# Layer 1 attention masks: from TensorE transposes of loaded tiles to a casting DMA and a transposing DMA

## Chip, cores and metric

The kernel runs on one core of one Trainium2 chip. The metric is the device time of one execution in microseconds (us). Most executions of one kernel agree within 0.3%. The profile is one execution, recorded by the hardware profiler.

Engines are named as in the profile: PE is TensorE (PEld its weight loads), DVE is VectorE, ACT is ScalarE, POOL is GpSimd, SP is SyncE. SP issues most DMAs; POOL issues the indirect ones. Both kinds run on the core's 16 DMA engines.

## The reference, cut to what matters

The model has two layers over `x` (32 batches, 512 nodes, 256 features) and a 0/1 adjacency `adj` (32, 512, 512, int32). Layer 0 is a mean aggregation over `adj` and a feed forward with a max-plus part; layer 1 is a graph attention and a slice mixer. The change is in layer 1's attention:

```
h = einsum("bnd,hde->bhne", nodes, W)                        # 4 heads of 64
e_src, e_dst = (h * a_src), (h * a_dst) summed per type t
weight = sum over t of (node_adj == t + 1) * (e_src[..., :, None] + e_dst[..., None, :])
weight = leaky_relu(weight, 0.01)
weight = where(node_adj == 0, -1e9, weight)
attention = softmax(weight, axis=-1)
dst = einsum("bhij,bhje->bhie", attention, h) + bias
out = layer_norm(relu(dst) + h)
```

With an adjacency of zeros and ones only one type counts, and the softmax is a masked sum: a row i adds over those j where adj[i, j] is 1. The kernel keeps j on the partitions, so it needs the adjacency turned: `mask[j, i] = adj[i, j]`.

## The kernel before, in words

**The fast path and its check.** `tile_kernel` runs `layer0_sorted` and, interleaved with its end, `layer1_plain`. Both assume something of the data and note in the tile `over` where it does not hold. At the end `over` is summed, read into a register as `rows`, and if it is above zero, both layers are computed again by general versions (L2206 to L2208). Layer 1's assumptions on the adjacency are two: it holds zeros and ones only, and no row is empty.

**Order of the work.** The code is written as Python generators that yield between pieces; `woven` and `braid` interleave them. A scheduler then orders the instructions on each engine's queue; each engine takes its queue strictly in order. Layer 0 begins with `features` (a chain of small DVE steps on the feed forward's weights) woven with `convs(0)`, the aggregation of the first 8 batches. Each batch loads four adjacency tiles through SP (L393), POOL turns them into floats (L394), and the layer norm of a batch takes an inverse root on POOL (`deviation`, L30 and L31) before DVE (L46) and ACT (L57) go on. When the features and the first segment are done, the feed forwards begin; layer 1's constants are set up between them (`following`), and from about 2450 us on layer 1 runs alone.

**Layer 1.** `attentions` handles one batch after the other: `attention(b)` is woven with `prepare(b + 1)`, by the counts TURNS - 4 (10) and STEPS (15). These also enter PACE, by which the whole stream is mixed with `mixer`, the second half of the layer, in pairs of batches. `prepare(b)` gathers the batch's nodes by POOL's indirect DMA (L1156), brings in the mask, normalises, turns x (`turned`), computes h and the exponentials (L1182 to L1188), and at its end writes a row per head to DRAM and reads it back broadcast to all partitions (`ownd`, `own`: L1199, L1202, on SP). `weigh` (L1215, DVE) multiplies the larger of `own` and `other` by the mask; `attention` feeds the result to PE (L1248, L1255).

**The mask before.** `masks(b)` loads four tiles of 128 rows (`ai`, int32, two buffers) through SP. For each, ACT makes one pass that casts to bf16 and sums each row (L1095), and a second that squares and sums (L1096). PE turns the four 128x128 blocks of the bf16 tile (`maskp`, L1086), DVE writes them into the mask as uint8 (L1087). The row sums lie in `edges`: the sum of squares equals the sum for zeros and ones, and a sum below 0.5 is an empty row. `masks(0)` runs while layer 0 still works; the others in `prepare(b)`.

Of the kernel before, what the change touches and what calls it, by code (L numbers as in the profile page):

```python
# [10 lines left out]
I32 = mybir.dt.int32  # L11
BF16 = mybir.dt.bfloat16
U32 = mybir.dt.uint32
AF = mybir.ActivationFunctionType
ALU = mybir.AluOpType
# [4 lines left out]
P = 128  # L20
N = 512
D = 256
NT = N // P
# [843 lines left out]
def layer1_plain(tc, ident, eps, x2s, ranks, adj, w, out, over, ps):  # L867
# [3 lines left out]
    nc = tc.nc  # L871
    B = adj.shape[0]
    SEG = B // len(x2s)
    GB = 2
    AH, _, HO = w["W"].shape
# [13 lines left out]
    HE = HO + 1  # L889
    AP = AH // 2  # L890
    TURNS = AP * NT + 6
    STEPS = 15
    WANTED = 68
    AHEAD = 3
    ATT = 2 * (AHEAD + 2) + AP + 1
# [7 lines left out]
    with ExitStack() as ctx:  # L903
        cst = ctx.enter_context(tc.tile_pool(name="c1", bufs=1, side="right", reuse_waits="tile"))
        dr = ctx.enter_context(tc.tile_pool(name="d1", bufs=2, space=DRAM))

        def ctile(name, shape):
            return cst.tile(shape, F32, tag=name, name=name)
# [8 lines left out]

        ones = ctile("ones", [P, P])
        nc.gpsimd.memset(ones, 1.0)
        identb = cst.tile([P, P], BF16, tag="identb", name="identb")  # L920
        nc.vector.tensor_copy(identb, ident)

        wa = ctile("wa", [P, DC, AH * HO + 2 * AH])
        for c in range(DC):
# [17 lines left out]
                                 start=c == 0, stop=c == DC - 1)  # L942
            nc.vector.tensor_scalar(over[:, : 2 * AH], pn[:, : 2 * AH], SMALL, None, ALU.is_gt)
        yield
        edges = ctile("edges", [P, 2, B * NT])
        abias = const("abias", [P, AH * HO], w["gnn_bias"].rearrange("h e -> (h e)").partition_broadcast(P))
        gamma = const("gamma", [P, AH * HO], w["ln_gamma"].rearrange("h e -> (h e)").partition_broadcast(P))
        beta = const("beta", [P, AH * HO], w["ln_beta"].rearrange("h e -> (h e)").partition_broadcast(P))
# [121 lines left out]
            nc.scalar.activation(ebsl, ebsl, AF.Exp)  # L1070

        se = ctx.enter_context(tc.tile_pool(name="e1", bufs=2, side="right", reuse_waits="tile"))
        masked = {}

        def masks(b, bank="any"):

            a, raw = [], []

            def load(t):
                raw.append(se.tile([P, N], I32, tag="ai", name=f"ai{b}_{t}", bufs=2))  # L1080
                nc.sync.dma_start(raw[t], adj[b, t * P : (t + 1) * P, :])

            def turn(t):
                pt = ps.tile([P, NT, P], BF16, tag=bank, name=f"maskp{b}_{t}")
                for j in range(NT):
                    nc.tensor.transpose(pt[:, j, :], a[t][:, j * P : (j + 1) * P], identb)  # L1086
                nc.vector.tensor_copy(mask[:, :, t * P : (t + 1) * P], pt)  # L1087

            load(0)
            load(1)  # L1090
            yield
            for t in range(NT):
                n = b * NT + t
                a.append(se.tile([P, N], BF16, tag="a", name=f"a{b}_{t}", bufs=3))
                nc.scalar.activation(a[t], raw[t], AF.Identity, accum_out=edges[:, 0, n : n + 1])  # L1095
                nc.scalar.activation(raw[t], raw[t], AF.Square, accum_out=edges[:, 1, n : n + 1])  # L1096
                if t + 2 < NT:
                    load(t + 2)
                if t == 1:
                    mask = se.tile([P, NT, N], mybir.dt.uint8, tag="mask", name=f"mask{b}")  # L1100
                    yield
                if t > 1:
                    turn(t - 2)
                    yield
            for t in range(NT - 2, NT):
                turn(t)
                yield
            masked[b] = mask

        yield from masks(0, "mm")  # L1110
        yield True
        ps = ctx.enter_context(tc.tile_pool(name="p1", bufs=4, space=PSUM, reuse_waits="tile"))
        sb = ctx.enter_context(tc.tile_pool(name="s1", bufs=2, reuse_waits="tile"))
# [9 lines left out]
        def normed(xt, xn, name):  # L1123

            mv = sb.tile([P, NT, 2], F32, tag="mv" + name[0], name=f"mv{name}")
            for t in range(NT):
                st = sb.tile([P, 6], F32, tag="st" + name[0], name=f"st{name}_{t}", bufs=4)
                nc.vector.bn_stats(st, xt[:, t, :])
                nc.vector.bn_aggr(mv[:, t, :], st)
            rs = sb.tile([P, NT], F32, tag="rs" + name[0], name=f"rs{name}")  # L1130
            deviation(nc, rs, mv[:, :, 1], eps)
            shift = sb.tile([P, NT], F32, tag="shift" + name[0], name=f"shift{name}")
            nc.vector.scalar_tensor_tensor(shift, mv[:, :, 0], -1.0, rs, ALU.mult, ALU.mult)
            for t in range(NT):
                nc.scalar.activation(xn[:, t, :], xt[:, t, :], AF.Identity, bias=shift[:, t : t + 1],
                                     scale=rs[:, t : t + 1])
# [13 lines left out]
        def prepare(b):  # L1150

            while b >= AHEAD_X and b - AHEAD_X not in stored:
                yield True
            xt = xs[b] = sb.tile([P, NT, D], F32, tag="x", name=f"x{b}", bufs=AHEAD_X)
            for t in range(NT):
                nc.gpsimd.indirect_dma_start(  # L1156
                    out=xt[:, t, :], out_offset=None, in_=x2s[b // SEG],
                    in_offset=bass.IndirectOffsetOnAxis(
                        ap=ranks[:, b * NT + t : b * NT + t + 1].bitcast(U32), axis=0))

            hv = sb.tile([P, NT, AH, HE], F32, tag="hv", name=f"hv{b}")
            xn = hv.rearrange("p t h e -> p (t h e)")[:, : NT * D].rearrange("p (t d) -> p t d", t=NT)
            edged = masks(b) if b not in masked else range(3)
            for i, _ in enumerate(edged):
                if i < 3 or b not in masked:
                    yield
                if i == 2:
                    normed(xt, xn, f"c{b}")
                    nc.gpsimd.tensor_add(xt, xt, beta.unsqueeze(1).to_broadcast([P, NT, D]))
                    yield  # L1170
            mask = masked.pop(b)
            xnT = yield from turned(xn, "x3T", f"x3T{b}")
            yield


            ht = sb.tile([P, NT, AH * HO], F32, tag="ht", name=f"ht{b}")
            other = sb.tile([P, NT, AH], F32, tag="other", name=f"other{b}")
            mine = sb.tile([P, AH, NT], F32, tag="mine", name=f"mine{b}")
            for t in range(NT):
                ph = psum("any", f"hp{b}_{t}")  # L1180
                for c in range(DC):
                    nc.tensor.matmul(ph[:, : AH * (HO + 2)], xnT[:, c, t * P : (t + 1) * P], wa[:, c, :],  # L1182
                                     start=c == 0, stop=c == DC - 1)
                d = ph[:, AH * HO : AH * HO + AH]
                nc.scalar.activation(mine[:, :, t], ph[:, AH * (HO + 1) : AH * (HO + 2)], AF.Exp, scale=1.0 - SLOPE)
                nc.scalar.activation(hv[:, t, :, HO], d, AF.Exp)
                nc.scalar.activation(other[:, t, :], d, AF.Exp, scale=SLOPE - 1.0)
                nc.scalar.copy(ht[:, t, :], ph[:, : AH * HO])  # L1188
                yield

            nc.gpsimd.tensor_add(hv[:, :, :, :HO], ht.rearrange("p t (h e) -> p t h e", h=AH),
                                 abias.rearrange("p (h e) -> p h e", h=AH).unsqueeze(1).to_broadcast([P, NT, AH, HO]))
            yield
            pt = psum("any", f"minep{b}")
            nc.tensor.transpose(pt[: AH * NT, :P], mine.rearrange("p h t -> p (h t)"), ident)
            row = sb.tile([AH * NT, P], F32, tag="turned", name=f"turned{b}", bufs=1)
            nc.scalar.copy(row, pt[: AH * NT, :P])
            own_row = dr.tile([AH, N], F32, tag="own", name=f"ownd{b}")
            nc.sync.dma_start(own_row.rearrange("h (t p) -> (h t) p", p=P), row)  # L1199
            own = [wide("own", f"own{b}_{h}", AH + 1) for h in range(AH)]  # L1200
            for h in range(AH):
                nc.sync.dma_start(own[h], own_row[h].partition_broadcast(P))  # L1202
            for t in range(NT):
                nc.vector.tensor_mul(hv[:, t, :, :HO], hv[:, t, :, :HO], hv[:, t, :, HO:].to_broadcast([P, AH, HO]))
            ready[b] = mask, ht, hv, other, own
            yield
# [11 lines left out]
        def attention(b):  # L1218

            mask, ht, hv, other, own = ready[b]  # L1220
            xt = xs[b]
# [46 lines left out]
            yield  # L1268
            dt = back(dT, "dp")
            rs = sb.tile([P, NT, AH], F32, tag="rs", name=f"rs{b}")  # L1270
            nc.vector.tensor_scalar_max(rs, dt.rearrange("p (t h e) -> p t h e", t=NT, h=AH)[:, :, :, 0], 1e-30)
            nc.vector.reciprocal(rs, rs)
            for q in range(AP):
# [325 lines left out]


        flags = over[:, 2 * AH + 3 :]
        nc.vector.tensor_sub(flags, edges[:, 1, :], edges[:, 0, :])
        nc.vector.tensor_scalar(flags, flags, 0.0, None, ALU.not_equal)
        nc.vector.tensor_scalar(edges[:, 0, :], edges[:, 0, :], 0.5, None, ALU.is_lt)
        nc.vector.tensor_add(flags, flags, edges[:, 0, :])


def layer1(tc, ident, eps, x2, adj, w, out):
# [632 lines left out]
```

## Time and profile before

| | |
|---|---|
| median of 3 runs | 4578.43 us (4575.21 to 4583.15) |
| profiled run | 4587.94 us |
| span of the profile (first to last instruction) | 4586.1 us |
| mean granted TensorE clock | 0.943 |
| layer 1, from 2530 to 4485 us | 1955 us |
| one batch of layer 1, by the distance of the ownd stores | about 63 us |

Lines of the profile that give the kernel's state besides those of the next part:

```profile
PE   5567988889988899878997999999999999999987
...
DVE  6668888887788877777775777777777777777763
ACT  2344565556655555555664444544544444554432
```

Each digit is the busy share of one fortieth of the span, in tenths. Layer 0's opening is the three slices on the left; layer 1 alone starts at about the 22nd. An idle engine costs nothing as such: what counts is which engine or DMA the others wait for in that stage.

### The profile page before, as it was taken

The page shows a single profiled execution, that of the slowest core. Times are in us where ns is not written, and L with a number is a line of the kernel's source. Part 1 is how long each engine was busy: PE and PEld are TensorE (multiplying, and loading weights), DVE is VectorE, ACT ScalarE, POOL GpSimd, SP SyncE. Part 2 cuts the span into 40 slices and gives each one's busy share as a digit, 9 for nine tenths or more (in the row PEclk, how much of TensorE's full clock was granted, in tenths as well). Part 3 has the DMA queues.
Part 4 walks back from the last instruction along what each step waited for, and adds up shares of the span by engine and source line. Part 5 has one row for each costly group of instructions (what it writes and reads, how often), then busy time and mean ns, then how long its engine had stood idle before and what let it go on. Part 6 is the DMA issues. An engine that isn't in the chain of part 4 may idle for free.

```text
span 4586.1 us, 56206 instructions
## 1 busy us (share of the span) xinstructions
PE 4011.0 (87%) x19287; PEld 2462.2 (54%) x19287; DVE 3391.6 (74%) x7008; ACT 2296.8 (50%) x4756; POOL 1743.1 (38%) x2036
## 2 busy tenths in 40 slices
PE   5567988889988899878997999999999999999987
PEld 4444655556556566445554355555555555555555
DVE  6668888887788877777775777777777777777763
ACT  2344565556655555555664444544544444554432
POOL 2356544654535644353423233222232333322210
PEclk8778999999999999989998999999999999999998
DMA  4447533654436543464422111111111111111100
GB/s 135 155 141 224 179 125 118 203 185 141 142 116 197 182 148 119 121 225 158 140 89 69 35 54 47 56 53 41 47 47 51 54 56 54 53 49 56 40 15 15
DMA packets 235100, 474.09 MB, mean 103 GB/s; under 512 B 38299, under 2 KB 114075, under 8 KB 234804
## 3 DMA queue, kind: packets, MB, share of 16 engines
q0 software_dynamic: 80256, 282.38, 19.2%
q1 hardware_dynamic: 154548, 188.02, 13.2%
q8 instruction: 154, 2.52, 0.2%
q14 instruction: 142, 1.16, 0.1%
HBM read 413.16 MB, written 57.16 MB: 103 GB/s over the span
## 4 chain that ended last, share of the span: by engine, by line
PE 28%; DVE 25%; DMA 7%; POOL 7%; issue 7%; ACT 4%; DVEq 0%; POOLq 0%; SPq 0%; ACTq 0%
DVE att L1215 4%; PE avp L1248 3%; PE clsp L625 3%; PE gatep L625 3%; DVE acc L639 2%; DMA rows<-table,xs 2%; DVE sw L1338 2%; PE po L654 2%; PE yTp L1348 2%; DVE sw L1343 2%; PE adp L1255 2%; DVE sst L1341 2%; PE oTp L1536 1%; PE xp L1401 1%; PE zp L1394 1%
## 5 line engine op out<-in xcount | busy, mean ns | idle before, releaser
L625 PE MATMUL clsp<-xnT,wc 128*128 128x512 f32 x1024 | 535.7, 643 | 83.8 <-ACT cls L627 53.2
L625 PE MATMUL gatep<-xnT,wg 128*128 128x512 f32 x1024 | 505.2, 613 | 13.8 <-ACT gate L627 13.5
L654 PE MATMUL po<-wd,acc 128*128 128x256 f32 x2048 | 458.5, 383 | 10.1 <-DVE h L410 7.2
L1215 DVE SCALAR_TENSOR_TENSOR att<-own,other,mask 128x512 f32<-128x512 f32 x512 | 392.3, 791 | 71.9 <-DMA own<-ownd 71.9
L654 PEld LDWEIGHTS po<-wd,acc 128*128 128x128 f32 x2048 | 391.4, 192 | 78.0 <-issue 11.1
L639 DVE SCALAR_TENSOR_TENSOR acc<-past,fld,acc 128x512 f32<-128x512 f32 x448 | 353.8, 794 | 34.0 <-ACT past L638 25.9
L600 DVE SCALAR_TENSOR_TENSOR best<-rows,xs,best 128x1024 f32<-128x1024 f32 x212 | 275.2, 1302 | 127.2 <-ACT best L594 71.5
L625 PEld LDWEIGHTS gatep<-xnT,wg 128*128 128x128 f32 x1024 | 199.5, 199 | 263.2 <-issue 205.7
L638 ACT ACTIVATE past<-tz,fld 128x512 f32<-128x512 f32 x448 | 291.4, 693 | 78.9 <-DVE acc L639 78.0
L597 POOL DMA_INDIRECT rows<-table,xs x212 | 255.3, 1204 | 166.2 <-DVE best L600 117.1
L625 PEld LDWEIGHTS clsp<-xnT,wc 128*128 128x128 f32 x1024 | 187.6, 203 | 241.0 <-issue 125.1
L634 ACT ACTIVATE acc<-tz,fld 128x512 f32<-128x512 f32 x256 | 198.8, 778 | 229.8 <-PE tz L632 229.4
L1348 PE MATMUL yTp<-sw,x 128*128 128x512 f32 x512 | 262.8, 650 | 57.4 <-DVE sw L1343 54.5
L1248 PE MATMUL avp<-att,hv 128*64 128x512 f32 x1024 | 305.0, 618 | 2.3 <-DVE att L1215 2.3
L436 PE MATMUL pm<-h,adj 128*128 128x258 f32 (+1 forms) x1024 | 180.4, 323 | 111.3 <-DVE keep L441 36.1
L1301 POOL TENSOR_TENSOR mu<-mu,eps 128x16 f32<-128x16 f32 x32 | 113.3, 3540 | 389.8 <-DVE mu L1300 389.7
L627 ACT ACTIVATE cls<-clsp,fld 128x512 f32<-128x512 f32 x256 | 175.7, 686 | 160.2 <-DVE acc L643 76.2
L1336 PE MATMUL lgp<-wsl,x4T 128*128 128x512 f32 x512 | 243.9, 610 | 9.3 <-ACT sw L1337 4.3
L1156 POOL DMA_INDIRECT x<-x2s,ranks x128 | 134.0, 1047 | 293.2 <-DVE att L1215 129.5
L627 ACT ACTIVATE gate<-gatep,fld 128x512 f32<-128x512 f32 x256 | 175.6, 686 | 136.5 <-PE gatep L625 102.1
L555 POOL DMA_INDIRECT xs<-rows_of,order x128 | 154.8, 1209 | 231.9 <-DVE acc L639 99.2
L1568 PE MATMUL outp<-v,swT 128*128 128x256 f32 x1024 | 227.6, 381 | 0.0
(599 smaller groups left out, 8943.0 us busy)
## 6 DMA issues: line engine op xcount, KB each, us to landing
adji<-in_adj SPq DMA_DIRECT2D x128, 256.0 KB
ai<-in_adj SPq DMA_DIRECT2D x128, 256.0 KB
own<-ownd SPq DMA_DIRECT2D x128, 256.0 KB
rows_of<-keep SPq DMA_DIRECT2D x32, 550.0 KB
x<-in_x SPq DMA_DIRECT2D x32, 512.0 KB
x2s<-xs SPq DMA_DIRECT2D x32, 512.0 KB
out<-x SPq DMA_DIRECT2D x32, 512.0 KB
rows<-table,xs POOLq DMA_INDIRECT x212
```

What stands on the lines that cost most here:

```text
L597: nc.gpsimd.indirect_dma_start(out=row, out_offset=None, in_=table, in_offset=bass.IndirectOffsetOnAxis(ap=idxs[:, k : k + 1].bitcast(U32) ...
L600: nc.vector.scalar_tensor_tensor(m, row, vals[:, k : k + 1], m, ALU.add, ALU.max)
L625: nc.tensor.matmul(pf, wf[:, c, f * P : (f + 1) * P], xnT[:, c, :], start=c == 0, stop=c == DC - 1)
L627: nc.scalar.activation(o, pf, fn, bias=fld[:, f, bf : bf + 1], scale=1.0 if fn == AF.Gelu else 0.5)
L638: nc.scalar.activation(r, z, AF.Relu, bias=fld[:, f, AT + b : AT + b + 1])
L639: nc.vector.scalar_tensor_tensor(y, r, fld[:, f, CH + b : CH + b + 1], y, ALU.mult, ALU.add)
L654: nc.tensor.matmul(po[:, i, :], acc[f][:, t * P : (t + 1) * P], wd[:, f, :], start=f == 0, stop=f == FC - 1)
L1215: nc.vector.scalar_tensor_tensor(e, own[h], other[:, j, h : h + 1], mask[:, j, :], ALU.max, ALU.mult)
L1248: nc.tensor.matmul(pv[q][k * HO : (k + 1) * HO, :], hv[:, j, h, :HO], weighed[b, h, j], start=j == 0, stop=j == NT - 1)
L1336: nc.tensor.matmul(pf, xnT[:, c, t * P : (t + 1) * P], wsl[:, c, :], start=c == 0, stop=c == DC - 1)
L1348: nc.tensor.matmul(py, xn[:, t, c * P : (c + 1) * P], sw[:, t, :], start=t == 0, stop=t == NT - 1)
L1568: nc.tensor.matmul(po[:, :D], swT[:, k, t * P : (t + 1) * P], v[:, k, :], start=k == 0, stop=k == KC - 1)
```

## The change

The adjacency of a batch is cast to bf16 by a DMA that POOL issues (`shorten`), from DRAM to DRAM, and brought into SBUF turned by a transposing DMA that SP issues (`turn`). The mask is bf16 instead of uint8. In place of ACT's two passes for each tile there is one Square pass for each batch over the whole mask with a bias of -0.5 (its result goes into a buffer that is overwritten later): each zero and each one gives 0.25, so the sum for a partition is 0.25 x 4 x 512. Empty rows are found from the attention's denominators: a denominator that is not above zero. TensorE's transposes, their PSUM tiles, DVE's casts and the bf16 identity are gone. `prepare` has 12 yields instead of 15, and STEPS follows.

```diff
-    STEPS = 15
+    STEPS = 12
...
-        def masks(b, bank="any"):
-            a, raw = [], []
-            def load(t):
-                raw.append(se.tile([P, N], I32, tag="ai", name=f"ai{b}_{t}", bufs=2))
-                nc.sync.dma_start(raw[t], adj[b, t * P : (t + 1) * P, :])
-            def turn(t):
-                pt = ps.tile([P, NT, P], BF16, tag=bank, name=f"maskp{b}_{t}")
-                for j in range(NT):
-                    nc.tensor.transpose(pt[:, j, :], a[t][:, j * P : (j + 1) * P], identb)
-                nc.vector.tensor_copy(mask[:, :, t * P : (t + 1) * P], pt)
...
-                nc.scalar.activation(a[t], raw[t], AF.Identity, accum_out=edges[:, 0, n : n + 1])
-                nc.scalar.activation(raw[t], raw[t], AF.Square, accum_out=edges[:, 1, n : n + 1])
...
-        yield from masks(0, "mm")
+        short, masked = {}, {}
+        def shorten(b):
+            if b < B:
+                short[b] = dr.tile([N, N], BF16, tag="short", name=f"short{b}", bufs=3)
+                nc.gpsimd.dma_start(short[b], adj[b], max_dma_last_dim=8192)
+        def turn(b):
+            if b < B:
+                masked[b] = se.tile([P, NT, N], BF16, tag="mask", name=f"mask{b}")
+                nc.sync.dma_start_transpose(masked[b], short.pop(b))
+        for b in range(2):
+            shorten(b)
+            yield
+        turn(0)
         yield True
...
-            edged = masks(b) if b not in masked else range(3)
-            for i, _ in enumerate(edged):
...
+            if b:
+                turn(b)
+            shorten(b + 2)
+            yield
+            yield
+            yield
+            normed(xt, xn, f"c{b}")
...
             ht = sb.tile([P, NT, AH * HO], F32, tag="ht", name=f"ht{b}")
+            nc.scalar.activation(ht.rearrange("p t e -> p (t e)").bitcast(BF16), mask.rearrange("p t n -> p (t n)"),
+                                 AF.Square, bias=centre, accum_out=edges[:, b : b + 1])
...
             rs = sb.tile([P, NT, AH], F32, tag="rs", name=f"rs{b}")
+            nc.vector.tensor_scalar(edges[:, B + b * NT : B + (b + 1) * NT],
+                                    dt.rearrange("p (t e) -> p t e", t=NT)[:, :, 0], 0.0, None, ALU.is_le)
...
-        nc.vector.tensor_sub(flags, edges[:, 1, :], edges[:, 0, :])
-        nc.vector.tensor_scalar(flags, flags, 0.0, None, ALU.not_equal)
-        nc.vector.tensor_scalar(edges[:, 0, :], edges[:, 0, :], 0.5, None, ALU.is_lt)
-        nc.vector.tensor_add(flags, flags, edges[:, 0, :])
+        nc.vector.tensor_copy(flags, edges[:, B:])
+        nc.vector.scalar_tensor_tensor(flags[:, :B], edges[:, :B], 0.25 * NT * N, flags[:, :B],
+                                       ALU.not_equal, ALU.add)
```

More of the change, by code (lines that the diff above doesn't have):

```diff
@@ L919, in layer1_plain @@
         nc.gpsimd.memset(ones, 1.0)
-        identb = cst.tile([P, P], BF16, tag="identb", name="identb")
-        nc.vector.tensor_copy(identb, ident)
         wa = ctile("wa", [P, DC, AH * HO + 2 * AH])
@@ L944, in layer1_plain @@
         yield
-        edges = ctile("edges", [P, 2, B * NT])
+        edges = ctile("edges", [P, B + B * NT])
+        centre = ctile("centre", [P, 1])
+        nc.gpsimd.memset(centre, -0.5)
         abias = const("abias", [P, AH * HO], w["gnn_bias"].rearrange("h e -> (h e)").partition_broadcast(P))
@@ L1072, in layer1_plain @@
         se = ctx.enter_context(tc.tile_pool(name="e1", bufs=2, side="right", reuse_waits="tile"))
-        masked = {}
-        def masks(b, bank="any"):
-            a, raw = [], []
-            def load(t):
-                raw.append(se.tile([P, N], I32, tag="ai", name=f"ai{b}_{t}", bufs=2))
-                nc.sync.dma_start(raw[t], adj[b, t * P : (t + 1) * P, :])
-            def turn(t):
-                pt = ps.tile([P, NT, P], BF16, tag=bank, name=f"maskp{b}_{t}")
-                for j in range(NT):
[L1086 to L1090, printed above, removed]
-            yield
[L1092 to L1108, printed above, removed]
-        yield from masks(0, "mm")
+        short, masked = {}, {}
[9 more added lines that the diff above has]
+            shorten(b)
+            yield
+        turn(0)
         yield True
@@ L1162, in prepare @@
             xn = hv.rearrange("p t h e -> p (t h e)")[:, : NT * D].rearrange("p (t d) -> p t d", t=NT)
-            edged = masks(b) if b not in masked else range(3)
-            for i, _ in enumerate(edged):
[L1165 to L1170, printed above, removed]
+            if b:
[5 more added lines that the diff above has]
+            normed(xt, xn, f"c{b}")
+            nc.gpsimd.tensor_add(xt, xt, beta.unsqueeze(1).to_broadcast([P, NT, D]))
+            yield
             mask = masked.pop(b)
```

## The prediction

> **What bounds the kernel now.** I read the page first: span, busy shares, DMA queues.
>
> ```profile
> PE 4011.0 (87%) x19287; PEld 2462.2 (54%) x19287; DVE 3391.6 (74%) x7008; ACT 2296.8 (50%) x4756; POOL 1743.1 (38%) x2036
> ```
>
> Then busy time by stage: the first 35 us, the rest of the opening (features and first segment), and layer 1 in its steady part. Columns are length, then busy us of PE, weight loads, DVE, ACT and POOL, then clock, DMA share, GB/s.
>
> ```profile
> 0.00:35.00 35.00, 7.76 (x27) 5.71 (x28) 13.78 (x26) 5.13 (x8) 11.27 (x59) 1.00 0.79 248
> 35.00:345.00 310.00, 194.62 (x903) 154.08 (x902) 219.57 (x801) 123.12 (x254) 120.35 (x290) 0.77 0.44 133
> 2530.00:4485.00 1955.00, 1834.39 (x10615) 1045.38 (x10613) 1426.79 (x3016) 925.47 (x2356) 550.19 (x411) 0.98 0.15 48
> ```
>
> The reader sees two different limits. Layer 1 is PE's (94% busy), DVE second, ACT half idle, DMA almost free. The opening is no engine's: it is short waits in turn, and in its first 35 us the DMA engines are what is full (0.79).
>
> Third, the groups that the change removes (busy us, mean ns):
>
> ```profile
> L1087 DVE CAST mask<-maskp 128x512 uint8<-128x512 bf16 x128 | 85.1, 674 | 2.5 <-PE maskp L1086 2.0
> L1096 ACT ACTIVATE ai<-ai 128x512 int32<-128x512 int32 x128 | 81.6, 639 | 1.3
> L1095 ACT ACTIVATE a<-ai 128x512 bf16<-128x512 int32 x128 | 80.4, 629 | 44.8 <-issue 29.5 <-DMA ai<-in_adj 13.1 <-PE maskp L1086 2.2
> L1086 PE MATMUL maskp<-identb,a 128*128 128x128 bf16 x512 | 46.1, 222 | 6.1 <-ACT sw L1337 3.9 <-DVE mask L1087 1.3 <-ACT a L1095 0.8
> ```
>
> Fourth, the chain of waits in one of layer 1's batches (start, us, what). It alternates: a stretch where DVE decides, then one where PE does.
>
> ```profile
> 3102.45 0.56 DVE mask L1087
> ...
> 3145.62 0.33 PE maskp L1086 x4
> ...
> 3161.19 0.67 PE maskp L1086 x12
> ```
>
> Adding the chain's pieces from 970 us to the end: L1087 30.4 us, L1086 15.5, L1095 with L1096 6.2; together 52.1.
>
> Last, POOL's opening, because the casts go to its queue:
>
> ```profile
> 23.73 0.61 POOL L394 CAST adj<-adji 128x512 fp32r<-128x512 int32 x1 [1.16 <-DMA adji<-in_adj]
> ...
> 27.00 1.27 POOL L394 CAST adj<-adji 128x512 fp32r<-128x512 int32 x2 [1.37 <-DMA adji<-in_adj]
> ...
> 33.93 1.01 POOL L31 TENSOR_TENSOR rsa<-rsa,eps 128x4 f32<-128x4 f32 x1
> ```
>
> POOL makes layer 0's adjacency (L394) and the norm's root (L31) within 35 us; DVE's next layer norm step (L46, 35.02 us) waits for that root, and all that is queued behind it on DVE, the features too, follows.
>
> **What the Trainium skill says.** "DMA: Bandwidth & Descriptors", section "SWDGE vs HWDGE vs iDMA": a cast inside a DMA can only be issued from GpSimd, a transposing DMA only from SP or ACT. The trace has neither. The same page, "Issuing engines are not separate DMA queues": DMAs of all issuers run on the same 16 engines and interleave. The trace agrees: only SP's queue is active in the first 35 us and already fills 0.79. "VectorE: DVE Perf Modes", "The three transpose paths": 1309 ns for a 128x128 bf16 block by DMA; no run shows it yet.
>
> **The change, part by part.**
>
> *Where the casts stand.* I compared the instruction order of the built changed kernel with the old one. The casts depend on nothing but an input, the buffers in DRAM hold none of them back, and the scheduler puts all 32 of them among POOL's first 73 entries, ahead of layer 0's second adjacency. The diff, which writes them into each batch's preparation, does not show this. Eight may be in flight: cast n+8 waits on POOL until cast n has landed. Read off that order: the first rsa (L31) stands behind the landing of cast 8, adj tiles 2 and 3 behind cast 14, the second rsa behind cast 23, the next adj behind cast 24. POOL's issue itself is some 32 x 1.0 us (an indirect DMA takes 1047 ns at L1156), inside those waits.
>
> *Price of a cast (c).* It reads 1.05 MB and writes 0.52 MB. The fullest slices of the opening move 339 to 346 GB/s. Reading alone sets the pace: 1.05/345 = 3.0 us, the lower end. Read and write both count: 1.57/345 = 4.6 us, which I take, as source and target are both in DRAM. The conversion halves the rate: 9.1 us, the upper end; nothing in the trace shows a converting DMA.
>
> *The opening.* The second rsa ends at 34.9 us now. Afterwards: 4 us to the first cast, 0.79 x 35 = 27.7 us of DMA work that the opening needs anyway on the same engines, 23 x 4.6 = 105, and 1 for L31: about 138. That is 103 late. Some waits vanish in it because their loads will have landed (high 4.4 us, sl 1.5): -6. So +97 (62 with c = 3.0; 201 with 9.1). The last 8 casts (36 us of DMA) run beside the feature loads and may add up to 25; I take 0 and keep it for the range. Nothing hides this: PE, DVE and ACT take their queues in order and each has batch 1's layer norm in front of the features; the first feed forward needs both.
>
> *Layer 1, removed.* PE 46.1 us, DVE 85.1, ACT 80.4 + 81.6 plus 25.0 + 25.9 of accumulator reads = 212.9, and 128 loads of 256 KB. Of that 52.1 lay on the chain. What is late next where DVE's cast goes is the next DVE instruction; where PE's turns go, the next matmul. Bounds: 25, if the other engine takes up half; 86, if the freed DVE and ACT also take a third from PE's 120.6 us of idle time (46 + 40).
>
> *Layer 1, added.* 32 ACT squares over 2048 elements: 128x1024 takes 1057 ns at L1297, so about 2.0, with the read 0.2: 70 us in all, 143 less than removed; cover is ACT's 53% idle time; without it up to 2 us each. 32 comparisons on DVE of about 0.15 us: 5, taken as on the chain. The multiplication at L1215 reads bf16 for uint8, with two f32 operands as before (791 ns; L639, all f32, 794): 0. Gain 52 - 5 = 47.
>
> *Transposing DMA.* It stands on SP just ahead of the previous batch's own rows: turn(b+1) before own(b), and waits until DVE's last att of b-1 frees the mask buffer. Queued behind it are ownd and own, and att of b waits for those. The slack is there now:
>
> ```profile
> 3164.88 0.73 DVE L1215 SCALAR_TENSOR_TENSOR att<-own,other,mask 128x512 f32<-128x512 f32 x1
> ```
>
> ```profile
> 3186.80 0.33 SPq L1199 DMA_DIRECT2D ownd<-turned  x1
> ```
>
> 21 us here, 14 to 35 over the batches after the second. Lower end: 0.5 MB at 345 GB/s, 1.5 us; upper: 16 blocks x 1.309 = 21 us (estimate from the page named). Either fits nearly everywhere: 0, at worst 25 in all.
>
> *The rest.* STEPS 15 to 12 keeps the weave, since the preparation now has 12 yields: 0, with 10 either way. The check's sum is exact in f32 (2048 x 0.25 = 512), so the branch that repeats both layers stays untaken.
>
> **Sum.** +97 - 47 = +50. The profiled run took 4587.9 (span 4586.1), giving 4638; the median of the three runs is 4578.4, 9.5 lower, so 4628.
>
> **Rivals.**
> A, faster: the opening has room. If casts go at c = 3.0 and 20 us of the delay are taken up by later DMA waits of the features (wraw 14.3, every 8.0), it costs 42; with a gain of 86 the time is 4534, with 60, 4560. For it: DMA is at 0.44 after 35 us. Against: those waits are for new transfers, not for old ones.
> B, slow conversion: c of 9.1 or more, +201 + 25 - 47: 4757. For it: an unknown unit converts. Against: nothing in the profile.
> C, the transpose is late: from about 20 us per transpose on, own waits; at 30 us roughly 8 x 32 = 250 more: 4880. Against: the slack above.
> D, the two parts cancel: c = 3.0 and gain 60: 4580.
>
> **How the numbers follow.** Forecast (c 3.0 to 7) 0.60; A 0.11; B 0.16; C 0.05; D 0.08. The measurement can tell about 0.2% (9 us). Faster 0.11, same 0.08, slower 0.81. The range runs from 4575, which lets A out, to 4745, short of B's middle and C: 8 in 10. The forecast's own range is 4593 to 4685.
>
> **What would show it.** Right: converting DMAs of 1 MB from 4 us on; DMA share near 1 for the first 100 us and more; DVE's second L46 at 130 to 140 instead of 35; layer 0 unchanged but shifted; layer 1 about 47 shorter, no maskp, ACT near 40%. Wrong: an unmoved second L46, DVE idle before att on own of more than the 71.9 us there now, or a layer 1 that isn't shorter.

## The result and the profile after

The changed kernel takes 4618.0 us (median of 4 runs, 4612.8 to 4628.7) against 4576.8 before: ratio 1.0094, 95% interval 1.0076 to 1.0113. The forecast was 4628. The profiled run took 4628.7, its span is 4627.0. The page's second part, busy time by engine:

```profile
PE 3952.5 (85%) x18775; PEld 2436.5 (53%) x18775; DVE 3326.7 (72%) x6909; ACT 2195.7 (47%) x4308; POOL 1770.5 (38%) x2069
```

Every engine but POOL has less to do than before, and the time is longer. The windows of the opening show where it goes (columns as in the prediction: length, busy us of PE, weight loads, DVE, ACT, POOL, clock, DMA share, GB/s). First the changed kernel, then the kernel before in the second of these stretches:

```profile
0.00:35.00 35.00, 0.00 (x0) 0.00 (x0) 9.35 (x14) 1.28 (x1) 11.36 (x60) 1.00 0.93 246
35.00:105.00 70.00, 10.88 (x36) 7.59 (x36) 3.83 (x14) 5.33 (x10) 15.72 (x30) 0.69 1.16 191
```

```profile
35.00:105.00 70.00, 45.63 (x220) 37.20 (x218) 57.86 (x247) 25.64 (x54) 16.89 (x52) 0.80 0.36 82
```

For 105 us the DMA engines are full (0.93, then 1.16: the share adds up the times of packets, so it can pass 1 where they overlap) and the engines that compute stand: DVE is busy for 3.8 us of 70 where it had 57.9. The trace's view of the casts (L1079) gives first and last start, what POOL waited for, and the time to landing:

```profile
L1079 POOL DMA_DIRECT2D short<-in_adj x32: 517/517/761, 3.7 to 104.1; - x32
  DMA short<-in_adj: 65.6, 23
DMA to landing us min/median/max: 7.3/22.9/37.6
```

All 32 leave in the first 104 us, and 23 of them wait on POOL for an earlier one. POOL's timeline shows the root of the second layer norm behind them; it ended at 34.9 us before:

```profile
98.99 0.52 POOL L1079 DMA_DIRECT2D short<-in_adj  x1 [1.75 <-DMA short<-in_adj]
...
102.19 1.05 POOL L31 TENSOR_TENSOR rsa<-rsa,eps 128x4 f32<-128x4 f32 x1
```

SP's loads for the features are late too. Its timeline after, then before:

```profile
62.48 0.37 SPq L200 DMA_DIRECT2D least<-ext  x1
...
81.33 0.34 SPq L202 DMA_DIRECT2D low<-least  x1
...
96.30 0.33 SPq L203 DMA_DIRECT2D high<-least  x1
```

```profile
30.78 2.50 SPq L200 DMA_DIRECT2D least<-ext  x2
...
40.76 0.33 SPq L202 DMA_DIRECT2D low<-least  x1
41.14 0.42 SPq L203 DMA_DIRECT2D high<-least  x1
```

One row is written to DRAM and read back. From the first store to the issue of `high` 10 us passed before, and 34 us now. DVE's wait for `high` grew from 4.4 to 14.1 us.

Layer 1 became shorter, by less than its engines were relieved. From the second to the last store of own rows, before and then after:

```profile
2512.00:4387.00 1875.00, 1763.95 (x10184) 995.40 (x10182) 1372.03 (x2894) 901.53 (x2319) 547.89 (x401) 0.98 0.16 50
```

```profile
2569.00:4428.00 1859.00, 1712.79 (x9699) 973.67 (x9700) 1320.19 (x2810) 807.48 (x1904) 561.04 (x408) 0.97 0.15 42
```

PE has 51 us less to do and DVE 52, but the stretch is 16 us shorter: PE's idle time rose from 111 to 146 us, DVE's from 503 to 539. (Another 13 us are won between the first and the second store.) No single wait of PE grew by the 35 us. The ones that grew most in these stretches, before and then after (PE's step and what it waited for; us in total, times, longest):

```profile
PE avp L1248 <- DVE att L1215: 2.3, 2, 2.1
PE hp L1182 <- ACT x3T L1145: 1.0, 3, 0.3
PE yp L1518 <- DVE mix L1511: 4.8, 5, 3.1
```

```profile
PE avp L1231 <- DVE att L1198: 16.7, 5, 8.6
PE hp L1165 <- ACT x3T L1125: 14.2, 3, 5.0
PE yp L1503 <- DVE mix L1496: 13.1, 14, 2.3
```

The two new operations of layer 1, from the views of their lines (count, duration in ns as min/median/max, first and last start; under the Square, what ScalarE waited for ahead of it, us and times):

```profile
L1085 SPq DMA_TRANSPOSE mask<-short x32: 1638/1954/2917, 2140.8 to 4343.2; - x32
DMA to landing us min/median/max: 4.2/4.3/7.5
```

```profile
L1158 ACT ACTIVATE ht<-mask,centre x32: 1987/2002/2004, 2545.0 to 4394.4; 128x2048 bf16<-128x2048 bf16 x32
  DVE mu L1284: 36.9, 26
```

The transposes land in 4.3 us. The Square takes 2.0 us as estimated, and has a wait that I had not seen: it writes into the hidden-row buffer, which DVE's second reduction (L1284) of two batches before still reads.

The lateness against the kernel before at fixed marks makes the ledger (us, from the starts of the same instructions in both traces; the runs are those of the next part):

| mark | before at | after | castonly | copyonly | cast16 | held | spread |
|---|---|---|---|---|---|---|---|
| fourth L46 on DVE | 103.1 | +81.0 | +79.3 | +74.2 | +36.4 | +3.2 | -1.7 |
| first L639 (feed forward) | 321.1 | +79.9 | +78.7 | +72.5 | +35.6 | +1.2 | -12.4 |
| 441st L639 | 2435.3 | +70.7 | +73.1 | +58.3 | +24.0 | -3.7 | +8.0 |
| first store of own rows | 2493.5 | +70.2 | +74.0 | +58.5 | +23.5 | -5.1 | +7.5 |
| last store of own rows | 4386.8 | +41.6 | +65.5 | +58.7 | +20.6 | -19.4 | -19.7 |
| span | 4586.1 | +40.9 | +61.5 | +55.3 | +21.7 | -19.3 | -20.9 |

So 81 us are lost in the opening and 29 won in layer 1 in the changed kernel. Between the marks of layer 0 single profiles drift by some 10 us in kernels that changed nothing there; no cause is read from these. The stretch of own rows varies as much: castonly, with layer 1 as before, comes out 9 us shorter there.

### The profile page after: what moved, and what is told of

It reads as the page before. It is cut to its first block, busy times and chain, and to the rows that moved or that the text cites. A ratio compares the mean times of both kernels' runs of the same rounds, so it can differ in the third digit from the quotient of the medians.

```text
span 4627.0 us, 54427 instructions
## 1 busy us (share of the span) xinstructions
PE 3952.5 (85%) x18775; PEld 2436.5 (53%) x18775; DVE 3326.7 (72%) x6909; ACT 2195.7 (47%) x4308; POOL 1770.5 (38%) x2069
## 4 chain that ended last, share of the span: by engine, by line
PE 35%; DVE 16%; issue 7%; DMA 7%; POOL 7%; ACT 4%; DVEq 0%; POOLq 0%; ACTq 0%; SPq 0%
PE yTp L1333 4%; PE avp L1231 4%; PE clsp L625 3%; PE gatep L625 2%; DMA rows<-table,xs 2%; PE adp L1238 2%; DVE acc L639 2%; PE outp L1553 2%; DVE att L1198 2%; DVE sw L1323 2%; PE po L654 2%; PE oTp L1521 2%; PE lgp L1321 1%; PE xp L1386 1%; DVE sw L1328 1%
## 5 line engine op out<-in xcount | busy, mean ns | idle before, releaser
L1198 DVE SCALAR_TENSOR_TENSOR att<-own,other,mask 128x512 f32<-128x512 f32 x512 | 371.0, 753 | 13.8 <-DMA own<-ownd 13.3
L639 DVE SCALAR_TENSOR_TENSOR acc<-past,fld,acc 128x512 f32<-128x512 f32 x448 | 354.5, 796 | 29.9 <-ACT past L638 22.4
L1231 PE MATMUL avp<-att,hv 128*64 128x512 f32 x1024 | 280.4, 616 | 16.8 <-DVE att L1198 16.7
L1136 POOL DMA_INDIRECT x<-x2s,ranks x128 | 146.6, 1146 | 296.1 <-DVE x L1555 149.3
L436 PEld LDWEIGHTS pm<-h,adj 128*128 128x128 f32 x1024 | 150.6, 212 | 171.6 <-issue 72.4
```

The costliest lines, as they stand in the source:

```text
L436: nc.tensor.matmul(pm[:, : c1 - c0], a[:, i, t * P : (t + 1) * P], h[:, i, c0:c1], start=i + c0 == 0, stop=i + 1 == NT and c0 > 0)
L639: nc.vector.scalar_tensor_tensor(y, r, fld[:, f, CH + b : CH + b + 1], y, ALU.mult, ALU.add)
L1198: nc.vector.scalar_tensor_tensor(e, own[h], other[:, j, h : h + 1], mask[:, j, :], ALU.max, ALU.mult)
L1231: nc.tensor.matmul(pv[q][k * HO : (k + 1) * HO, :], hv[:, j, h, :HO], weighed[b, h, j], start=j == 0, stop=j == NT - 1)
```

## The experiments

My theory at first: the opening's delay is the casts' alone, and what layer 1 wins is separate from it, so the two add up. The rivals: casts cost as much wherever they stand; or what layer 1 wins is only slack that any late start gives back. All ratios below are to the kernel before on the same chip, with the 95% interval.

**The casts held back into layer 1 (held).**

```diff
-                nc.gpsimd.indirect_dma_start(
+                gather = nc.gpsimd.indirect_dma_start(
...
-                nc.gpsimd.dma_start(short[b], adj[b], max_dma_last_dim=8192)
+                with tc.issue_after(behind) if behind is not None else ExitStack():
+                    nc.gpsimd.dma_start(short[b], adj[b], max_dma_last_dim=8192)
...
-            shorten(b + 2)
+            shorten(b + 2, gather.ins)
```

> Casts of batches 2 to 31 are issued behind the node gather of the batch two before, as the source writes them; casts 0 and 1 stay at the start. Nothing else is changed. Theory (the opening's wait and layer 1's gain are two separate things that add up): DVE's fourth L46 within 10 us of its 103.1 us before instead of 184.1, layer 1 still about 40 us shorter in sum, time 4535 to 4545, ratio to before about 0.991. Rival 1 (a cast on POOL's queue inside layer 1 holds up the gathers and POOL's norms behind it, 1 to 2 us for each batch on the path): 4560 to 4600. Rival 2 (the 40 us won back after the opening are slack that any late start would give back): no gain without the late start, 4570 to 4585.

Measured: 4569.2 us, ratio 0.999 (0.998 to 1.0001). The opening is back (+3.2 at the fourth L46), but from the first to the last store of own rows only 14 us are won and not 29, and by the ratio the whole kernel wins 5 us or nothing. The theory, 4535 to 4545, misses. The second rival isn't settled by this run, as the interval reaches 1.0001; the run with spread casts, below, settles it. The first one holds in size (4560 to 4600 was its range), though its place, the gathers, isn't shown: what grew most in the trace are PE's waits for DVE's `sw` (L1328), from 59 to 68 us over layer 1.

**The casts alone (castonly).** The kernel before, with this ahead of layer 1:

```diff
+        for b in range(B):
+            short = dr.tile([N, N], BF16, tag="short", name=f"short{b}", bufs=3)
+            nc.gpsimd.dma_start(short, adj[b], max_dma_last_dim=8192)
```

> The kernel before, with the 32 casts added in front of layer 1's preparation, where the scheduler lifts them to the start; their results are not read. Theory: the whole opening delay of 81 us belongs to the casts and lasts to the end, since nothing of layer 1 is taken away: 4650 to 4665, ratio about 1.017. Rival 2 (later slack absorbs a late start): 4615 to 4630, ratio about 1.009, the same as with the whole change.

Measured: 4653.5 us, ratio 1.0172 (1.0142 to 1.0202), 79 us by the ratio. The fourth L46 is 79.3 us late, with the whole change 81.0. The opening's delay is the casts' alone, and a late start gives little back: the theory holds. What the change wins after the opening is then 1.0094 less 1.0172, or 36 us, uncertain by some 16.

**The same bytes without a conversion (copyonly).**

```diff
-            short = dr.tile([N, N], BF16, tag="short", name=f"short{b}", bufs=3)
-            nc.gpsimd.dma_start(short, adj[b], max_dma_last_dim=8192)
+            short = dr.tile([3 * N // 4, N], I32, tag="short", name=f"short{b}", bufs=3)
+            nc.gpsimd.dma_start(short, adj[b, : 3 * N // 4, :], max_dma_last_dim=8192)
```

> The same as the run with the casts alone, but each cast is a plain DRAM to DRAM copy of 384 rows: 0.79 MB read and 0.79 MB written, 1.57 MB in all as in the cast, without a conversion. If read and written bytes set the price (what I took for 4.6 us a cast), the delay is as with the casts, 75 to 85 us, 4650 to 4665. If reading alone sets it, 0.79 of 1.05 MB gives about three quarters of the cast's part, a delay of 55 to 65 us, 4630 to 4645. If the conversion costs extra, less than 50 us, under 4630.

Measured: 4644.1 us, ratio 1.0156 (1.0133 to 1.0178), a delay of 71 us, at the fourth L46 74. That lies between two of the three branches (75 to 85 us if read and written bytes set the price, 55 to 65 if reading alone does), though the time itself stands in the second one's range, and the interval reaches into both; only the third, under 50 us for a dear conversion, is out. The traces say more. Summed over their first 150 us, the packets of POOL's queue hold the 16 DMA engines for 94.8 us in castonly, 3.0 for each cast, and for 78.4 us here, 2.45 for each copy. So the cast takes a fifth longer for the same sum of bytes; whether for the conversion or because it reads more of them isn't told apart. The pages of the kernel before, castonly and copyonly also show what the profile counts as bytes moved:

```profile
DMA packets 235100, 474.09 MB, mean 103 GB/s; under 512 B 38299, under 2 KB 114075, under 8 KB 234804
```

```profile
DMA packets 239709, 490.88 MB, mean 106 GB/s; under 512 B 38811, under 2 KB 114587, under 8 KB 239412
```

```profile
DMA packets 238685, 499.26 MB, mean 108 GB/s; under 512 B 38811, under 2 KB 114587, under 8 KB 235316
```

The casts add 16.8 MB and the copies 25.2, which is 32 times what each writes (0.52 and 0.79 MB). A transfer counts once, by what it writes. This run also shows something that I had not asked for. The view of the copies' line:

```profile
L1075 POOL DMA_DIRECT2D short<-in_adj x32: 507/507/752, 3.8 to 105.3; - x32
  DMA short<-in_adj: 5.4, 3
```

POOL waits for landings for 5.4 us only, not for 64.5 as in castonly, and the second L46 comes at 63.2 us, not at 101.5. Yet the opening ends about as late. In the list of waits of its first 140 us (us in total, times, longest) stand loads that SP issued:

```profile
POOL adj L394 <- DMA adji<-in_adj: 49.3, 8, 22.1
...
DVE top L204 <- DMA high<-least: 28.6, 1, 28.6
```

The place on POOL's queue is therefore not what sets the delay. The 16 DMA engines are (share 0.90 in the first 35 us of this run and 0.99 in the next 70), which every load of the opening needs, whoever issued it, as the Trainium skill's "DMA: Bandwidth & Descriptors", "Issuing engines are not separate DMA queues", has it. The trace before, with SP's queue alone in its first 35 us, could not show that; this one does.

**Half the casts (cast16).** As castonly, with `range(B // 2)`.

> The kernel before with 16 casts instead of 32 at the start, results not read. Theory (the DMA engines are full until the last cast has landed, and the opening ends that much later: 79 us for 32 casts is 2.5 us a cast): fourth L46 35 to 45 us late, time 4610 to 4620, ratio about 1.009. Rival 1 (what counts is that the roots stand behind the casts on POOL's queue; with 16 the first stands behind one wait and the second behind none): 15 us or less, under 4595. Rival 2 (a fixed cost of saturation, small loads late whatever the number): more than 60 us, over 4635.

Measured: 4608.4 us, ratio 1.0071 (1.0056 to 1.0087); the fourth L46 is 36.4 us late, inside the theory's range (the time is 2 us below its own). Half the casts, about half the delay: 2.3 us for each of the first 16, 2.7 for each of the others. Both rivals fall.

**Casts spread over layer 0 (spread).** Each cast is tied behind the fourth adjacency conversion of a batch in layer 0, from batch 8 on:

```diff
-                nc.gpsimd.tensor_copy(a[:, t, :], ai)
+                turn_ = nc.gpsimd.tensor_copy(a[:, t, :], ai)
+            for k in ([b - 8] if b >= 8 else []) + ([b] if b >= 24 else []):
+                with tc.issue_after(turn_.ins):
+                    nc.gpsimd.dma_start(SHORT[k], adj[k], max_dma_last_dim=8192)
```

> The changed kernel with each cast tied behind layer 0's fourth adjacency conversion of a batch: casts 0 to 7 behind batches 8 to 15 and so on, the last eight batches with two casts each. None stands in the opening and none in layer 1. Theory (layer 1's gain with the casts out of the way is the 29 us that the trace of the changed kernel shows from the first to the last ownd store, and holding the casts inside layer 1 gave half of it back): 4540 to 4555, ratio about 0.994. Rival 1 (32 casts of 1 MB disturb layer 0's gathers from the table as much as the opening): 4575 to 4600. Rival 2 (layer 1's gain exists only with the late start): 4570 to 4580.

Measured: 4561.4 us, ratio 0.9966 (0.9951 to 0.998): faster than the kernel before, by 16 us. That is short of the theory's range and better than both rivals'. Its layer 1 wins 27 us between the first and the last store of own rows, about as the changed kernel's (29), without a late start: the second rival falls. With the casts free it would have been the 36 us of the ratios; the trace shows where some of the rest may be: in layer 0 it goes from 8 us ahead at the 121st L639 to 8 behind at the 321st, the stretch in which 20 of the 32 casts stand. That fits the first rival in part; one profile doesn't prove it. (The diff leaves out the DRAM buffers, one for each batch, and that `shorten` is gone. Three casts, from 231 to 293 us, still start before the first feed forward at 309.)

**What takes back part of layer 1's gain?** By the prediction's sum the relief of PE and DVE was worth 47 us, and the trace shows 29 (the ratios, 36 with 16 either way, leave the gap open). Four edits to the changed kernel ask why less came.

*The Square with a buffer of its own (dump)* and *without the Square (nosq)*, which leaves the check for zeros and ones out:

```diff
-            nc.scalar.activation(ht.rearrange("p t e -> p (t e)").bitcast(BF16), mask.rearrange("p t n -> p (t n)"),
+            waste = se.tile([P, NT * N], mybir.dt.uint8, tag="waste", name=f"waste{b}", bufs=1)
+            nc.scalar.activation(waste, mask.rearrange("p t n -> p (t n)"),
                                  AF.Square, bias=centre, accum_out=edges[:, b : b + 1])
```

```diff
+        nc.gpsimd.memset(edges[:, :B], 0.25 * NT * N)
...
-            nc.scalar.activation(ht.rearrange("p t e -> p (t e)").bitcast(BF16), mask.rearrange("p t n -> p (t n)"),
-                                 AF.Square, bias=centre, accum_out=edges[:, b : b + 1])
```

> The changed kernel, with the checking Square writing into a small buffer of its own (uint8) instead of into the buffer of the hidden rows, so that it no longer waits for DVE's second reduction of the batch two before (36.9 us of ACT waiting in the trace, 26 times). Theory (this wait is part of why layer 1 won about 30 us and not the 50 us that TensorE's busy time fell by): 4600 to 4610. Rival (ACT has room, the wait costs nothing): 4613 to 4623, no difference.

> The changed kernel without the Square pass: the check for zeros and ones is left out, its sums are set to the value that a valid mask gives. Theory (ScalarE's 70 us of squares lie in its idle time, as I predicted): 4610 to 4625, no difference from 4618. Rival (each square holds ScalarE's queue for 2.2 us plus its wait for the hidden-row buffer, ahead of the copies that the next products wait for, and that is why layer 1 won 29 instead of 47 us): 4590 to 4605.

Measured: dump 4644.5, ratio 1.0152 (1.0129 to 1.0175), slower than the changed kernel by 26 us; nosq 4627.5, ratio 1.0116 (1.01 to 1.0132), no gain over 1.0094. Leaving the pass out wins nothing, so ScalarE's room covers it. That dump lost is a miss for its theory and its rival. Its list of waits has ScalarE waiting 44 us, 13 times, for the transposing DMA, as the Square moved up in ScalarE's order. I took that for the cause and tried it.

*The Square later (late).* The pass stands behind the copy of the turned row, with the same small buffer.

> The changed kernel with the Square moved behind the batch's turned row and into a small buffer of its own, so that it waits for neither the hidden-row buffer nor the transposing DMA. Theory (what made the run with an own buffer slower, 4644, was the Square standing early in ScalarE's queue and waiting 44 us for the mask): 4605 to 4620. Rival (any shift of ScalarE's order costs, whatever the Square waits for): 4630 to 4650.

Measured: 4648.5, ratio 1.0158 (1.0139 to 1.0177). Slow again, inside the rival's range, but it told nothing apart: without the tie to the hidden-row buffer the scheduler moves the pass up to where its mask lands, wherever it is written. The fourth batch's Square starts at 2621 us in dump and 2612 in late, and at 2657 in the changed kernel, with the own rows of all three within some 10 us. ScalarE waits 44.1 us for the transposing DMA here too:

```profile
ACT waste L1182 <- DMA mask<-short: 44.1, 13, 5.8
```

So this wait remains the candidate for what makes both slow; that it costs the 26 to 30 us was not shown.

*The old count of steps (pace).* Three empty yields, and STEPS 15 again:

```diff
-    STEPS = 12
+    STEPS = 15
...
+            for _ in range(3):
+                yield
             mask = masked.pop(b)
```

> The changed kernel with the preparation's old count of yields: three empty yields where TensorE's turns were, and STEPS 15, so PACE is 0.887 again instead of 0.795. Theory (the mix of the two streams is worth 10 us either way, as I took it): 4608 to 4628. Rival (the smaller PACE puts the mixer's short chains back to back, which is the 27 us by which TensorE's idle time in layer 1 grew): 4590 to 4605.

Measured: 4651.6, ratio 1.0176 (1.0154 to 1.0198). Its theory (10 us either way) and its rival (faster) are both wrong: it is 38 us slower than the changed kernel by the ratios, and as slow as the kernel before with the casts alone (1.0172), which still does all the mask work. In the old weave the removed work was worth nothing that the intervals can tell. The windows of layer 1 and the list of PE's waits, first of castonly, then of pace (whose profiled run took 4666.8 us, 15 more than its median):

```profile
2586.00:4452.00 1866.00, 1750.11 (x10184) 989.82 (x10182) 1367.91 (x2893) 900.54 (x2319) 550.45 (x401) 0.99 0.16 50
```

```profile
PE yTp L1351 <- DVE sw L1346: 56.2, 37, 2.4
...
PE yp L1521 <- DVE mix L1514: 4.8, 5, 3.1
```

```profile
2573.00:4470.00 1897.00, 1734.74 (x9709) 983.33 (x9710) 1338.40 (x2816) 815.59 (x1907) 565.48 (x403) 0.97 0.14 41
```

```profile
PE yTp L1335 <- DVE sw L1330: 46.1, 34, 2.4
PE yp L1505 <- DVE mix L1498: 35.4, 14, 3.1
PE yTp L1335 <- DVE sst L1329: 30.9, 10, 4.4
```

PE's waits for the mixer's steps on DVE (`mix`, `sst`) hold some 60 us that weren't there (`sst` had 0.8); those for `sw` are 10 less. PE idles for 162 us in place of 116. I read that as the removed work having stood where PE waits now, so that taking it away turned work into waiting; no run tests that by itself.

None of these edits tests the granted TensorE clock. In the windows shown it is 0.98 before, 0.97 in the changed kernel and in pace, 0.99 in castonly, and over whole executions 0.932 to 0.943 in all runs with the new mask against 0.941 to 0.950 in all with the old one. If all of PE's 1713 us in the changed kernel's stretch followed the clock (a rough estimate), 0.97 in place of 0.98 would cost some 17 us, and 0.97 in place of 0.99 in pace against castonly some 35. So part of the gain that is missing, and of the gain that the removed work seems not to bring in pace, may have gone into a lower clock. Why it is lower isn't shown. It doesn't explain the steps: pace and the changed kernel have the same 0.97 and lie 38 us apart.

**The new count of steps with the old work (before12).** Is it then the tighter weave alone that wins?

```diff
-    STEPS = 15
+    STEPS = 12
...
-                if i < 3 or b not in masked:
+                if i < 3:
                     yield
```

> The kernel before, with all of its mask work (loads, ACT passes, turns, casts), but with the last three steps of it put into the step after the layer norm: 12 yields and STEPS 12, the changed kernel's weave. Theory (the mask work itself was hidden; the changed kernel with the old weave, 4652, is as slow as the old kernel with the casts alone, 4653, so what won 35 us in layer 1 is the tighter weave): 4540 to 4555. Rival (the weave wins only where the work is gone, as the steps then really become shorter): 4570 to 4590 or slower.

Measured: 4618.6, ratio 1.0082 (1.0062 to 1.0101): 38 us slower. The theory falls. PE's list of waits from the second to the last store of own rows shows that it now waits for the mask work, which it hardly did before (3.9 and 1.0 us for these two):

```profile
PE maskp L1086 <- ACT sw L1337: 30.0, 11, 3.9
PE lgp L1336 <- DVE mask L1087: 20.2, 5, 5.5
```

With the casts' 1.0172 taken off where they stand at the start, the four corners are (us against the kernel before, from the ratios; the left column is good to some 9 us, the right one to some 17):

| | mask work as before | mask work on the DMA engines |
|---|---|---|
| 15 steps | 0 | +2 |
| 12 steps | +38 | -36 |

Neither edit wins anything by itself. The gain comes only when the number of steps shrinks with the work in them. The +38 belongs to this one way of fitting the old work into 12 steps, with the last three pieces together in one; another spread of the pieces was not tried.

**Fewer steps still (spread10).** The spread casts, with two of the three empty yields at the start of `prepare` out and STEPS 10.

> The run with spread casts, with two of the three empty yields at the start of the preparation taken out as well and STEPS 10. Theory (each empty step costs layer 1 some 10 us, as three of them cost 33): 4535 to 4550, ratio about 0.993. Rival (12 is where the streams fit by chance; fewer steps bring the node gathers too close to the layer norm that waits for them): 4565 to 4600.

Measured: 4554.8, ratio 0.995 (0.9936 to 0.9965), the fastest of all; from the first to the last store of own rows 42 us are won, where spread won 27. The size is smaller than expected (4535 to 4550), and its interval overlaps spread's, so that 10 steps beat 12 isn't shown. In layer 0 this profile, too, goes from 6 us ahead at the 121st L639 to 11 behind at the 321st.

**Every transpose twice (turn2).**

```diff
+                nc.sync.dma_start_transpose(masked[b], short[b])
                 nc.sync.dma_start_transpose(masked[b], short.pop(b))
```

> The changed kernel with every transposing DMA issued twice into the same buffer, the second waiting on SyncE for the first (4.3 us from issue to landing in the trace), so that each batch's own rows leave SyncE 4 to 6 us later. Theory (14 to 35 us of slack between the last att of the batch before and the own rows, as I read it): 4610 to 4630, no difference from 4618. Rival (the squares and the own rows already wait for the mask, and each batch gets later by half of it or more): 4680 or more.

Measured: 4616.8, ratio 1.0089 (1.0073 to 1.0105), as the changed kernel. A second transpose of 4.3 us ahead of each batch's own rows costs nothing that the intervals can tell: in the trace, after the first batches, both have landed 5 us or more before SP issues the own rows, as the slack in the prediction had it.

## Why the prediction was right, and where its terms were off

The direction, the place and the sign of both large terms were right: the casts rise to the start and cost more there than layer 1 wins. The sum, +50, came out as +41 in the profiled run, from terms that were off in opposite ways. That the sum is so close is in part luck, since layer 1's gain hangs on a term that the prediction put at 0. Two of its signs of being right were missed: the second L46 came at 103.3 us and not at 130 to 140, and ACT is busy for 47% and not near 40%.

- *Where the casts stand*: right, all 32 by 104 us. The reading of POOL's queue held to the letter (the second root leaves after the 23rd landing), but as the cause it was only half of it. copyonly has the roots early and the opening as late; the DMA engines decide.
- *Price of a cast and the opening*: +97 forecast, +81 measured. The mis-sized term is 23 x 4.6. With the prediction's own 4 us and 27.7 us, 23 landings by 101.6 us leave 3.0 us for each, my lower end and also what a cast's packets hold the DMA engines for (94.8 / 32), so the second root ended at 103.2 and not at 138. The 4.6 added read and written bytes and divided by 345 GB/s, but that figure counts a transfer once, so the bytes of both sides were set against a rate for one. The opposite error lies behind the second root, where -6 was forecast with the last casts at 0: from the second to the fourth L46 the changed kernel needs 80.8 us and the old one 68.1, which is +13. Of that 10 is the wait for `high`, which was to vanish and grew, as its row is written and read back while the DMA engines are still full. Counted over all 32, a cast costs 2.5 us of delay (79.3 / 32).
- *Layer 1*: -47 forecast, -36 by the ratios (uncertain by 16), -29 in the trace between own-row stores. Inside the bounds of 25 to 86. Summing the removed instructions on the chain priced what was there, not what would stand there next: on PE it was small waits for many things (`att`, `x3T`, `mix`). The removal that it priced is worth about nothing in the old weave (pace), so that 36 lies near 47 is in good part luck. The lower clock named above is a cost that it had no term for; its size is open.
- *STEPS and PACE at 0, with 10 either way*: the step that failed. It is worth 38 us, in either direction: 38 slower without it in the changed kernel, 38 slower with it in the old one (placed as in before12). It passed unnoticed because the change made both edits together.
- *ScalarE's squares hidden*: right (nosq). *The transposing DMA hidden*: right (turn2). DVE's wait of `att` for own rows even fell, from 71.9 to 13.3 us; as it is 76.0 in pace with the same DMA, the fall comes with the number of steps.
- *The rivals*: B falls with copyonly, C with turn2. A and D needed casts at 3.0, which they were, but also took the last ones as free and layer 1's gain as 60 or more.

## What to carry to other kernels

A DMA that depends on nothing but an input goes wherever the scheduler puts it (here, to the start), and its bytes are paid by whoever needs the DMA engines then: look at the built order, and tie such a transfer to the stage that has room. When work was removed from one of the two interleaved streams here, it paid only with the steps that had held it removed too; price the two edits together and then try each alone. Time that leaves the chain of waits is not yet a gain: ask which wait ends last in its place.

## What the runs showed of the hardware

A cast of 1.05 to 0.52 MB inside a DMA delayed the opening about as much as a plain copy with the same 1.57 MB read and written: 79 us for 32, against 74. It held the 16 DMA engines somewhat longer, for 3.0 us against 2.45 (the 94.8 and 78.4 us of castonly and copyonly).

The transposing DMA brought 16 blocks of 128x128 bf16 in 4.3 us from issue to landing, 2.0 us of it on SP. The Trainium skill's "VectorE: DVE Perf Modes", "The three transpose paths", gives 1309 ns for one block, from which I had estimated 21 us at the upper end. The measurement decides: 16 blocks in one transfer took 3.3 times that figure and not 16 times.

DVE can be held by POOL. The Trainium skill's "SBUF — State Buffer", "Terms", says that the two share a pair of ports with an exclusive lock, and that the loser blocks. The trace of the changed kernel agrees: the same step takes 0.68 us where POOL does nothing beside it. POOL's timeline, then DVE's:

```profile
3530.32 2.38 POOL L1150 TENSOR_TENSOR x<-x,beta 128x1024 f32<-128x1024 f32 x1
```

```profile
3530.72 2.53 DVE L1328 TENSOR_TENSOR sw<-sw,sst 128x512 f32<-128x512 f32 x1
```

DVE's step ends 0.55 us after POOL's. It is no single case: this step runs 128 times, takes over 1 us in 10 of them, and all 10 lie beside the same addition on POOL (L1150) and end 0.55 or 0.56 us after it. In the kernel before, 28 of POOL's 32 additions made a DVE step longer than the median of its kind by more than 0.3 us, 56 us in all, and 28 did in the changed kernel, 58 us in all. What moved is where they fall: `att` had 13 of them before and has 3 now, the steps that make `sw` 15 and 24. In before12, with the old mask, it is 2 and 24, and in pace, with the new one, 22 and 6, so the place goes with the number of steps more than with the mask. What it is worth where they fall was not tried.
